# A transformer block in float32: three edits to the work of the first batch (fold constant in the prologue, xn of the next batch made and turned earlier, q scaled on GpSimd)

## The chip, the cores and the metric

The kernel runs on one core of one Trainium2 chip. A time is the device time of one execution in microseconds (us). Three runs of the kernel before gave 633.22, 635.14 and 635.72 us; the median, 635.14, is the time before. Another execution was taken with the profiler, and all rows shown here come from it.

## The reference

For x of shape 8 x 1024 x 256 (batches, tokens, channels), with 16 heads of 16 channels and a hidden layer of 1024:

```python
x  = L0_attn_x
xn = (x - mean(x)) / sqrt(var(x) + 1e-5)                    # over the 256 channels
# linear attention, no softmax
q, k, v = split(xn @ qkv_w + qkv_b)                         # 16 heads of 16
q, k = q / |q|, k / |k|                                     # per token and head
kv   = einsum('bhnd,bhne->bhde', k, v)
attn = einsum('bhnd,bhde->bhne', q, kv) @ proj_w + proj_b
# feed forward
ffn  = relu(xn @ W1 + b1) @ W2 + b2
out  = x + attn + ffn
```

Everything is float32.

## The kernel before

Batches are worked through one after the other, and each is software-pipelined with the next. A batch is 1024 tokens by 256 channels, which is eight tiles of 128 tokens.

*What is made of a batch.* `norm_stats`, `norm_scale` and `norm_apply` turn x into xn with tokens on the partitions. A turned copy `xnT`, with channels on the partitions, is made in one of two ways. For batch 0, TensorE transposes (`turn_on_pe`). For later batches `turn` (L289) is used: VectorE transposes 32 x 32 blocks into a tile `turn_x`, and DMA transfers then put the blocks where they belong. One call of `turn_x` (L304) does one of four such pieces: one VectorE transpose of 128 x 512 and four transfers of 64 KB. `project` makes q and k (products `pq`, L328, with the bias added on VectorE, L332). `norms` takes the inverse lengths and scales k on GpSimd (L464, called from `scale`); `scale_q` scales q by the same line.

*Attention without v.* v is never formed. `mix_g` (L497) multiplies the xn of a batch with its scaled k into `gp` (16 products, L502), and ScalarE copies it to `gT` (L507). `mix_kv` multiplies the v columns of `qkv_w` with `gT` (`kvp`, L516) and VectorE keeps the blocks on the diagonal (`kvm`, L522). `mix_m` multiplies with `proj_w` (`mp`, L533) into a 256 x 256 matrix M, which the second layer applies to the turned q, beside W2. The bias of v comes in by two small steps, done once. `shift` (L492) adds 1 to the first 128 channels of xn on ScalarE, and `fold_bias_of_v` (L479) changes the v columns of `qkv_w`: a product of a constant matrix `mean` (all 1/128) with these columns (`of_rows`, L485), a row `a` from it and from the bias (L487), and a sum of `a` into the columns (L490). The constant is filled by a VectorE memset (L483) in that function.

*The hidden layer.* The products of both layers use Strassen's scheme on 2 x 2 blocks, seven products for eight. In `hidden` (L543) each of four slices i has three steps: `first(i)` with the products a, c, d, `fifth(i)` with e, and `last(i)`, which adds a second product into a, d and e. Their names in the profile are `pha`, `phc`, `phd` and `phe` (L555). VectorE adds the intermediate sums u1, u2, u3 (L567) and ScalarE takes the relu (L562). GpSimd forms the sums of blocks that the second layer needs (`sums_of_h`, L188 to L192). A float32 product of 128 x 512 is two passes in the profile, hence two matmul records.

*What sets the order.* The kernel is written under a manual schedule: each engine executes its instructions in the order in which the Python code calls them, and waits by semaphore for the inputs, or for a buffer to come free. In `hidden` the twelve steps stand in a list: first(0), fifth(0), first(1), last(0), fifth(1), first(2), last(1), fifth(2), first(3), last(2), fifth(3), last(3), numbered 0 to 11. After step n come the sums of h that are due, and then the small work that a table names for n: `first_steps` (L635) for batch 0, `later_steps` for the others. So the table decides where the small products, the normalisation of the next batch and its turns stand in each engine's queue. In batch 0, the turns of batch 1 stand at steps 7, 8, 8 and 9. After `hidden(0)` come the transposes of q of batch 0 on TensorE (`tpq`, L283), GpSimd's sums of W2 (L184) and of q, `project(1)`, and then the second layer of batch 0, `second` (L684, products L679).

*Buffers that matter here.* The pool `one` has one buffer per tag. The tiles xn of all batches share the tag `xn`, so the next batch's xn may be written only when all readers of the last one, gp among them, are done. `mean`, `kvm` and `Mt` share the tag `Mt`. The PSUM tiles of the products share seven banks, taken in turn; a product that takes a bank waits until its last reader is done.

*Queues of transfers.* Nearly all transfers are issued by SyncE (SP), in order. The exception is the turns of batch 1: of the four transfers of each piece, the last is issued by ScalarE (`last`, L289 and L308).

Of the kernel before, what the change touches and what calls it, by code (L numbers as in the profile page):

```python
# [9 lines left out]
F32 = mybir.dt.float32  # L10
# [6 lines left out]
def kernel(  # L17
# [34 lines left out]
    nc = tc.nc  # L52
    P = 128
# [11 lines left out]
    R = P // S  # L65
# [7 lines left out]
    one = ctx.enter_context(tc.tile_pool(name="one", bufs=1))  # L73
# [16 lines left out]
    def bank(shape, name):  # L90

        return psum.tile(shape, F32, tag="bank", name=name)

    xs, xqs, xns, xnTs, xSs, hTs, qks, qTs, mixes, Ms, hSs = ({} for _ in range(11))
# [13 lines left out]
    def load_squares(b, halves=(0, 1)):  # L108
        xqs[b] = one.tile([P, 2, R, HT, CJ], F32, tag="xq", name=f"xq_{b}")
        for n in halves:  # L110
            for j in range(R):
                nc.sync.dma_start(out=xqs[b][ts(j, S), n], in_=squares_v(x, b, n, j))
# [51 lines left out]
    nc.vector.memset(eps_sb, LN_EPS)  # L164
    ones = const.tile([P, 1], F32, tag="ones", name="ones")
    nc.vector.memset(ones, 1.0)

    blk = const.tile([P, G], F32, tag="blk", name="blk")
    nc.vector.tensor_reduce(blk, ident.rearrange("p (g d) -> p g d", d=D), AX.X, ALU.add)
# [69 lines left out]
    def norm_stats(b, tiles):  # L239

        xt, n = xs[b], len(tiles)
        st = work.tile([P, NT, 6], F32, tag="st", name=f"st_{b}_{tiles[0]}")[:, :n, :]
        mv = small.tile([P, NT, 2], F32, tag="mv", name=f"mv_{b}_{tiles[0]}")[:, :n, :]
        for i, t in enumerate(tiles):
            nc.vector.bn_stats(st[:, i, :], xt[:, t, :])
        for i in range(n):
            nc.vector.bn_aggr(mv[:, i, :], st[:, i, :])
        rstd = small.tile([P, NT], F32, tag="rstd", name=f"rstd_{b}_{tiles[0]}")[:, :n]
        nc.scalar.activation(rstd, mv[:, :, 1], AF.Sqrt, bias=eps_sb)
        for i, t in enumerate(tiles):  # L250
            stats[b, t] = i, mv, rstd

    def norm_scale(b, tiles, on_act):
        i, mv, rstd = stats[b, tiles[0]]
        nc.vector.reciprocal(rstd, rstd)
        if on_act:
            nmr = small.tile([P, NT], F32, tag="nmr", name=f"nmr_{b}_{i}")[:, : len(tiles)]
            nc.vector.scalar_tensor_tensor(nmr, mv[:, :, 0], -1.0, rstd, ALU.mult, ALU.mult)
            for t in tiles:
                stats[b, t] += (nmr,)  # L260

    def norm_apply(b, tiles):
        if b not in xns:
            xns[b] = one.tile([P, NT, C], F32, tag="xn", name=f"xn_{b}")
        for t in tiles:
            xt, xn = xs[b][:, t, :], xns[b][:, t, :]
            i, mv, rstd, *nmr = stats.pop((b, t))
            if nmr:
                nc.scalar.activation(  # L269
                    xn, xt, AF.Identity, bias=nmr[0][:, i : i + 1], scale=rstd[:, i : i + 1]  # L270
                )
            else:
                nc.vector.tensor_scalar(
                    xn, xt, mv[:, i, 0:1], rstd[:, i : i + 1], ALU.subtract, ALU.mult
                )
# [10 lines left out]
                    tp.rearrange("p (u w) m -> p u w m", w=2),  # L286
                )

    def turn(dst, src, name, last=nc.sync):  # L289


        sq = one.tile([P, R, KC, NP, S, 2], F32, tag="turn", name=f"turn_{name}")
        src = src[:, :, 0:C].rearrange("p (u w) (k j s) -> p j k u w s", w=2, k=KC, s=S)
        for j in range(R):
            nc.vector.transpose(sq[:, j, :, :, :, :].rearrange("p k u s w -> p k u w s"), src[:, j])  # L295
            for r in range(R):
                (last if r == R - 1 else nc.sync).dma_start(
                    out=dst[ts(j, S), :, :, ts(r, S), :], in_=sq[ts(r, S), j, :, :, :, :]
                )
            yield  # L300

    turns = {}

    def turn_x(b):  # L304

        if b not in xnTs:
            xnTs[b] = big.tile([P, KC, NP, P, 2], F32, tag="xnT", name=f"xnT_{b}")
            turns["x", b] = turn(xnTs[b], xns[b], f"x_{b}", nc.scalar if b == 1 else nc.sync)  # L308
        next(turns["x", b])

    def project(b, between={}, with_norms=True):
# [42 lines left out]
    def norms(b, h, ss):  # L354
        invert(ss)
        scale(nc.gpsimd, b, h, 1)
# [104 lines left out]
    def scale(eng, b, h, s):  # L461

        part = qks[b][:, ts(h, HT), ts(s, C)].rearrange("p t (g d) -> p t g d", d=D)
        eng.tensor_tensor(  # L464
            part, part,
            norms_of[b, h, s].unsqueeze(3).to_broadcast([P, HT, H, D]), ALU.mult,
        )

    def scale_q(b, h):
        scale(nc.vector, b, h, 0)  # L470

    def turn_q(b):

# [5 lines left out]
    def fold_bias_of_v():  # L479

        wv = wqkv_sb[:, :, of_v]
        mean = one.tile([P, P], F32, tag="Mt", name="mean")
        nc.vector.memset(mean, 1.0 / P)  # L483
        of_rows = bank([P, C], "of_rows")
        nc.tensor.matmul(of_rows, mean, wv[:, 0, :], start=True, stop=True)  # L485
        a = one.tile([P, C], F32, tag="ksum", name="a")
        nc.vector.scalar_tensor_tensor(  # L487
            a, qkvb_sb[:, of_v], 1.0 / P, of_rows, ALU.mult, ALU.subtract
        )
        nc.vector.tensor_tensor(wv, wv, a.unsqueeze(1).to_broadcast([P, KC, C]), ALU.add)  # L490

    def shift(b):  # L492

        part = xns[b][:, :, 0:P]
        nc.scalar.activation(part, part, AF.Identity, bias=ones)

    def mix_g(b):  # L497
        qk, xn = qks[b], xns[b]
        gp = ps_mix.tile([P, KC, C], F32, tag="mix", name=f"gp_{b}")
        for f in range(KC):  # L500
            for t in range(NT):
                nc.tensor.matmul(  # L502
                    gp[:, f, :], xn[:, t, ts(f, P)], qk[:, t, C : 2 * C],
                    start=(t == 0), stop=(t == NT - 1),
                )
        gT = one.tile([P, KC, C], F32, tag="gT", name=f"gT_{b}")
        nc.scalar.copy(gT, gp)  # L507
        mixes[b] = gT

    def mix_kv(b):  # L510
        gT = mixes.pop(b)
        kvp = ps_mix.tile([P, KC, P], F32, tag="mix", name=f"kvp_{b}")
        for c in range(KC):
            cols = slice(2 * C + c * P, 2 * C + (c + 1) * P)
            for f in range(KC):
                nc.tensor.matmul(  # L516
                    kvp[:, c, :], wqkv_sb[:, f, cols], gT[:, f, ts(c, P)],
                    start=(f == 0), stop=(f == KC - 1),
                )
        kvm = one.tile([P, KC, P], F32, tag="Mt", name=f"kvm_{b}")  # L520
        for c in range(KC):
            nc.vector.tensor_tensor(  # L522
                kvm[:, c, :].rearrange("p (g d) -> p g d", d=D),
                kvp[:, c, :].rearrange("p (g d) -> p g d", d=D),
                blk.unsqueeze(2).to_broadcast([P, G, D]), ALU.mult,
            )
        mixes[b] = kvm

    def mix_m(b):
        kvm = mixes.pop(b)  # L530
        mp = ps_mix.tile([P, KC, C], F32, tag="mix", name=f"mp_{b}")
        for c in range(KC):
            nc.tensor.matmul(mp[:, c, :], kvm[:, c, :], projw_sb[:, c, :], start=True, stop=True)  # L533
        M = one.tile([P, KC, C], F32, tag="M", name=f"M_{b}")
        Mt = one.tile([P, 3, HC], F32, tag="Mt", name=f"Mt_{b}")
        Ms[b] = M, Mt
        nc.vector.tensor_copy(M, mp)
        sums_of_b(
            nc.gpsimd, [M[:, k, ts(m, HC)] for k in range(2) for m in range(2)],
            [Mt[:, i, :] for i in range(3)],  # L540
        )
# [93 lines left out]
    def first_steps(b):  # L635

        lo, hi = range(HT), range(HT, NT)
        return {
            0: [lambda: load_squares(b)] + [lambda h=h: norms(b, h, all_ss[b, h]) for h in range(2)],
            1: [lambda: norm_stats(b + 1, lo)],  # L640
            2: [lambda: shift(b), lambda: norm_stats(b + 1, hi), lambda: norm_scale(b + 1, lo, True)],
            3: [lambda: fold_bias_of_v()],
            4: [
                lambda: mix_g(b), lambda: norm_scale(b + 1, hi, False),
                lambda: norm_apply(b + 1, lo), lambda: scale_q(b, 0), lambda: scale_q(b, 1),
            ],
            5: [lambda: norm_apply(b + 1, hi)],
            6: [lambda: mix_kv(b)],
            7: [lambda: turn_x(b + 1)],
            8: [lambda: turn_x(b + 1), lambda: turn_x(b + 1)],  # L650
            9: [lambda: turn_x(b + 1)],
            10: [lambda: mix_m(b)],
            11: [lambda: load(b + 2)],
        }
# [236 lines left out]
```

## Time and profile before

| what | value |
|---|---|
| median of three runs | 635.14 us (633.22 to 635.72) |
| the profiled execution: its time | 633.63 us |
| the profiled execution: its span, first to last instruction | 631.8 us |
| mean granted clock of TensorE | 0.994 |
| TensorE busy | 616.4 us, 98% of the span |
| VectorE / ScalarE / GpSimd busy | 400.4 / 208.8 / 349.0 us |
| TensorE's share of the chain that ended last | 94% |

In the profile PE is TensorE, PEld its weight loads, DVE VectorE, ACT ScalarE, POOL GpSimd and SP SyncE. A row of the timeline has the start in us from the span's start, the length in us, the engine, the line of the kernel, the operation, out<-in by the program's names, the shapes, and how many instructions were merged. Brackets hold the idle time of the engine before the row, and what ended it. Lengths of merged matmuls include the tail of the last one, so the next matmul starts before a row's end. The chain of waits, the waits of an engine and the windows (busy time of each engine in a stretch, with the clock that TensorE was granted, 1.00 being full) are other views of the same execution.

### The profile page before, as it was taken

To read this page: it belongs to the slowest core of one execution; us is meant where nothing else is said; L and a number is where in the kernel's file an instruction comes from. 1 tells how busy PE (TensorE), PEld (TensorE's weight loads), DVE (VectorE), ACT (ScalarE), POOL (GpSimd) and SP (SyncE) were. 2 spreads that over 40 slices of the span, in tenths; PEclk is the share of its full clock that TensorE was granted. 3 is DMA by queue.
4 is the path that set the end of the run, shared out by engine and by line. 5 is a ranking of instruction groups with operands and counts; after the bars stand their busy time and mean duration, and the time that the engine had idled before them with its cause. 6 is when DMAs were issued, how large, how long until landed. Compare 5 with 4: busy or idle time off the path is not lost.

```text
span 631.8 us, 6102 instructions
## 1 busy us (share of the span) xinstructions
PE 616.4 (98%) x1843; PEld 346.4 (55%) x1843; DVE 400.4 (63%) x700; ACT 208.8 (33%) x348; POOL 349.0 (55%) x288
## 2 busy tenths in 40 slices
PE   8969899999999999999999999999999999999996
PEld 5445446448464475545664475644846547554454
DVE  6775553687466784577665875668746778417823
ACT  4324622343232521435214442325324252103500
POOL 3543875379702995239932599027970299513801
PEclk9979999999999999999999999999999999999999
DMA  7721300384005810158002750039200560004202
GB/s 243 141 41 22 112 1 0 78 184 73 0 7 127 168 33 1 31 125 164 14 1 58 149 126 0 2 94 192 49 0 12 122 124 11 0 0 101 66 0 66
DMA packets 139503, 43.26 MB, mean 68 GB/s; under 512 B 135880, under 2 KB 136272, under 8 KB 139472
## 3 DMA queue, kind: packets, MB, share of 16 engines
q1 hardware_dynamic: 138384, 42.63, 30.5%
q10 hardware_dynamic: 1088, 0.26, 0.2%
q8 instruction: 14, 0.23, 0.1%
q14 instruction: 17, 0.14, 0.1%
HBM read 19.80 MB, written 8.39 MB: 45 GB/s over the span
## 4 chain that ended last, share of the span: by engine, by line
PE 94%; DVE 3%; DMA 1%; ACT 0%; issue 0%; SPq 0%; DVEq 0%; ACTq 0%
PE poe L679 11%; PE poa L679 11%; PE pod L679 10%; PE gp L502 9%; PE phe L555 8%; PE phd L555 8%; PE pha L555 8%; PE poc L679 5%; PE pq L328 4%; PE phc L555 4%; PE pqd L396 3%; PE pqe L396 3%; PE pqa L396 3%; PE pqc L396 2%; PE kvp L516 1%; PE mp L533 1%
## 5 line engine op out<-in xcount | busy, mean ns | idle before, releaser
L716 POOL TENSOR_TENSOR xq<-xq,yt_o 128x512 f32<-128x512 f32 x30 | 37.9, 1264 | 180.9 <-DVE yt_o L711 180.9
L562 ACT ACTIVATE hT<-hT,b_sb 128x512 f32<-128x512 f32 x96 | 68.7, 721 | 63.4 <-DVE hT L567 59.1
L188 POOL TENSOR_TENSOR hS<-hT 128x512 f32<-128x512 f32 x31 | 46.1, 1489 | 68.6 <-issue 41.5
L555 PE MATMUL pha<-xnT,w_sb 128*128 128x512 f32 x128 | 65.4, 592 | 0.0
L374 ACT ACTIVATE sq<-qk 128x512 f32<-128x512 f32 x48 | 29.0, 629 | 109.1 <-DVE qk L402 59.1
L502 PE MATMUL gp<-qk,xn 128*128 128x256 f32 x256 | 58.0, 386 | 0.0
L679 PE MATMUL poa<-hT,w_sb 128*128 128x512 f32 x128 | 57.5, 592 | 0.0
L502 PEld LDWEIGHTS gp<-qk,xn 128*128 128x128 f32 x256 | 49.8, 195 | 11.0 <-issue 3.9
L567 DVE TENSOR_TENSOR hT<-phe,u 128x512 f32<-128x512 f32 x64 | 43.7, 683 | 6.2 <-PE phe L555 4.4
L711 DVE STREAM_TRANSPOSE yt_o<-y_o 128x512 f32<-128x512 f32 x30 | 33.0, 1099 | 16.2 <-ACT y_o L766 13.9
L190 POOL TENSOR_TENSOR hS<-hT,hS 128x512 f32<-128x512 f32 x31 | 39.9, 1286 | 2.4
L192 POOL TENSOR_TENSOR hT<-hT 128x512 f32<-128x512 f32 x31 | 40.9, 1321 | 0.0
L189 POOL TENSOR_TENSOR hS<-hS,hT 128x512 f32<-128x512 f32 x31 | 39.5, 1274 | 2.4
L567 DVE TENSOR_TENSOR u<-phc,u 128x512 f32<-128x512 f32 x32 | 21.8, 681 | 27.2 <-ACT u L581 18.1
L679 PEld LDWEIGHTS poa<-hT,w_sb 128*128 128x128 f32 x128 | 24.3, 190 | 25.0 <-issue 24.4
L295 DVE STREAM_TRANSPOSE turn_x<-xn 128x512 f32<-128x512 f32 x28 | 17.7, 685 | 31.3 <-ACT xn L269 31.3
L555 PEld LDWEIGHTS pha<-xnT,w_sb 128*128 128x128 f32 x128 | 23.8, 190 | 23.4 <-issue 21.0
L562 ACT ACTIVATE hT<-pha,b_sb 128x512 f32<-128x512 f32 x32 | 21.8, 682 | 36.8 <-PE pha L555 32.7
L555 PE MATMUL phe<-xS,w1t 128*128 128x512 f32 x64 | 33.6, 607 | 0.0
L581 ACT COPY u<-pha 128x512 f32<-128x512 f32 x32 | 18.4, 575 | 44.6 <-PE pha L555 43.9
L555 PE MATMUL phe<-xS,w_sb 128*128 128x512 f32 x64 | 32.7, 592 | 0.0
L555 PE MATMUL phd<-xnT,w_sb 128*128 128x512 f32 x64 | 32.7, 592 | 0.0
(165 smaller groups left out, 1189.9 us busy)
## 6 DMA issues: line engine op xcount, KB each, us to landing
xq<-in_L_attn_x_dram SPq DMA_DIRECT2D x60, 128.0 KB, 3.7
out_dram<-xq SPq DMA_DIRECT2D x60, 128.0 KB, 2.8
x<-in_L_attn_x_dram SPq DMA_DIRECT2D x14, 512.0 KB, 5.1
qT<-turn_q SPq DMA_DIRECT2D x112, 64.0 KB, 2.3
xnT<-turn_x SPq DMA_DIRECT2D x108, 64.0 KB, 2.1
x<-in_L_attn_x_dram SPq DMA_DIRECT2D x4, 256.0 KB, 4.5
w_sb<-in_L_ffn_W_dram SPq DMA_DIRECT2D x2, 512.0 KB, 7.4
w_sb<-in_L_ffn_W_dram SPq DMA_DIRECT2D x8, 128.0 KB, 3.1
```

The costliest lines, as they stand in the source:

```text
L188: eng.tensor_tensor(s1, a21, a22, ALU.add)
L189: eng.tensor_tensor(s2, s1, a11, ALU.subtract)
L190: eng.tensor_tensor(s4, a12, s2, ALU.subtract)
L192: eng.tensor_tensor(a21, a11, a21, ALU.subtract)
L396: nc.tensor.matmul(dst[:, w, :], a[:, g, :, w], rhs, start=start and w == 0, stop=stop, skip_group_check=True,)
L502: nc.tensor.matmul(gp[:, f, :], xn[:, t, ts(f, P)], qk[:, t, C : 2 * C], start=(t == 0), stop=(t == NT - 1),)
L555: nc.tensor.matmul(dst, lhsT, rhs, start=start, stop=stop, skip_group_check=True)
L562: nc.scalar.activation(block(i, n, m), src, AF.Relu, bias=b1_sb[:, fc : fc + 1])
L567: nc.vector.tensor_tensor(dst, p, q, ALU.add)
L679: nc.tensor.matmul(dst, l, r, start=start and n == 0, stop=stop and n == len(lhs) - 1, skip_group_check=True,)
L711: nc.vector.transpose(yt.rearrange("p u w r c -> p u r w c"), y.rearrange("p u (s r) w -> p u r w s", r=R),)
L716: nc.gpsimd.tensor_tensor(xh, xh, yt.rearrange("p u w r c -> p (u w) r c"), ALU.add)
```

## The change

The constant `mean` is filled in the prologue. In the table of batch 0, q is scaled at step 1 and on GpSimd (before: step 4, on VectorE); `fold_bias_of_v` moves from step 3 to step 4, behind fifth(1); at step 4 both halves of xn of batch 1 are written before `fold_bias_of_v` and `mix_g` are called (before: `mix_g` first, then the first half of xn, and the second half at step 5). The turns move from steps 7, 8, 8, 9 to 5, 5, 6, 7. All transfers of the turns are issued by SP.

```diff
@@ prologue
     nc.vector.memset(ones, 1.0)
+    mean = one.tile([P, P], F32, tag="Mt", name="mean")
+    nc.vector.memset(mean, 1.0 / P)
@@ turn
-    def turn(dst, src, name, last=nc.sync):
+    def turn(dst, src, name):
...
-                (last if r == R - 1 else nc.sync).dma_start(
+                nc.sync.dma_start(
@@ turn_x
-            turns["x", b] = turn(xnTs[b], xns[b], f"x_{b}", nc.scalar if b == 1 else nc.sync)
+            turns["x", b] = turn(xnTs[b], xns[b], f"x_{b}")
@@ scale_q
-        scale(nc.vector, b, h, 0)
+        scale(nc.gpsimd if b == 0 else nc.vector, b, h, 0)
@@ fold_bias_of_v
-        mean = one.tile([P, P], F32, tag="Mt", name="mean")
-        nc.vector.memset(mean, 1.0 / P)
@@ first_steps
-            1: [lambda: norm_stats(b + 1, lo)],
+            1: [
+                lambda: norm_stats(b + 1, lo), lambda: scale_q(b, 0), lambda: scale_q(b, 1),
+            ],
             2: [lambda: shift(b), lambda: norm_stats(b + 1, hi), lambda: norm_scale(b + 1, lo, True)],
-            3: [lambda: fold_bias_of_v()],
             4: [
-                lambda: mix_g(b), lambda: norm_scale(b + 1, hi, False),
-                lambda: norm_apply(b + 1, lo), lambda: scale_q(b, 0), lambda: scale_q(b, 1),
+                lambda: norm_scale(b + 1, hi, False), lambda: norm_apply(b + 1, lo),
+                lambda: norm_apply(b + 1, hi), fold_bias_of_v, lambda: mix_g(b),
             ],
-            5: [lambda: norm_apply(b + 1, hi)],
-            6: [lambda: mix_kv(b)],
+            5: [lambda: turn_x(b + 1), lambda: turn_x(b + 1)],
+            6: [lambda: mix_kv(b), lambda: turn_x(b + 1)],
             7: [lambda: turn_x(b + 1)],
-            8: [lambda: turn_x(b + 1), lambda: turn_x(b + 1)],
-            9: [lambda: turn_x(b + 1)],
             10: [lambda: mix_m(b)],
             11: [lambda: load(b + 2)],
```

## The prediction

> **What bounds the kernel now.** I read the page first, then the waits of the TensorE queue, then the timeline of each engine over the first batch, then the granted clock by microsecond. The page puts TensorE at 98% busy and 94% of the chain that ended last, so only a pause of TensorE, or slow running of it, can be won back. The waits of TensorE have two entries above 1.5 us, and both are in the first batch:
>
> ```profile
> PE of_rows L485 <- DVE mean L483: 5.5, 1, 5.5
> PE pq L328 <- DMA xnT<-turn_x: 1.9, 1, 1.9
> ```
>
> (engine, line, what it waited for: total us, times, longest.) The first is the small product of `fold_bias_of_v` (L485), held by the memset of its constant. The second is the first projection of batch 1, held by the transfers that turn its xn. Where they lie, from the timelines (start us, us, ...):
>
> ```profile
> 31.31 1.02 PE L555 MATMUL phe<-xS,w_sb 128*128 128x512 f32 x2
> 37.88 1.22 PE L485 MATMUL of_rows<-wqkv_sb,mean 128*128 128x256 f32 x2 [5.55 <-DVE mean L483]
> 40.60 8.50 PE L502 MATMUL gp<-qk,xn 128*128 128x256 f32 x32
> 48.94 1.02 PE L555 MATMUL pha<-xnT,w_sb 128*128 128x512 f32 x2
> ...
> 65.30 1.91 PE L283 MATMUL tpq<-ident,qk 128*128 128x128 f32 x16
> 69.12 3.25 PE L328 MATMUL pq<-wqkv_sb,xnT 128*128 128x512 f32 x7 [1.91 <-DMA xnT<-turn_x]
> ```
>
> ```profile
> 33.15 0.69 DVE L567 TENSOR_TENSOR u<-phc,u 128x512 f32<-128x512 f32 x1 [0.84 <-ACT u L581]
> ...
> 37.66 0.17 DVE L483 MEMSET mean<- 128x128 f32 x1
> ```
>
> The memset takes 0.17 us; it is late because VectorE works in order and it is behind the statistics of batch 1. The pause costs more than its length, as the granted clock shows (window, its length, busy us of PE, PEld, DVE, ACT, POOL with counts, then the clock):
>
> ```profile
> 36.00:37.00 1.00, 0.00 (x0) 0.00 (x0) 0.97 (x7) 0.74 (x2) 0.00 (x0) 0.83 0.00 0
> 37.00:38.00 1.00, 0.12 (x1) 0.12 (x1) 0.82 (x3) 1.00 (x3) 0.08 (x1) 0.50 0.00 0
> ...
> 43.00:44.00 1.00, 1.00 (x5) 0.82 (x5) 1.00 (x2) 0.00 (x0) 1.00 (x1) 0.76 0.00 0
> 44.00:45.00 1.00, 1.00 (x6) 0.90 (x5) 1.00 (x1) 0.00 (x0) 0.41 (x1) 1.00 0.00 0
> ...
> 69.00:70.00 1.00, 0.88 (x2) 0.51 (x3) 0.00 (x0) 1.00 (x3) 1.00 (x2) 1.00 0.94 373
> ```
>
> The clock falls to a half at about 36.7 us (0.83 in that window), and is whole again at about 43.75 (0.76). TensorE works from 37.88 on, so 5.88 us of its work run at half speed: 2.94 us lost. After the second pause of 1.91 us the clock is 1.00.
>
> **The change, step by step.**
>
> *The constant.* Its memset joins VectorE's prologue, where VectorE idles 1.82 us for x: 0.17 us at no cost. If that cover were gone it would cost 0.17.
>
> *TensorE up to the end of gp.* `fifth(1)` now comes ahead of the small product and waits for nothing: its two passes start at 31.31 + 0.86 = 32.17 and end their turn at 33.03 (0.43 a pass). The small product still needs a free PSUM bank. In the changed program that wait is for VectorE's u of `first(1)`: 33.15 + 0.69 = 33.84. So it starts at 33.88, and the pause is 33.88 - 33.03 = 0.85 us where it was 5.55. It took 1.01 (37.88 to the next pass at 38.89) at half clock; I take 0.55. gp would start at 34.43. Its other inputs are there: the keys scaled by GpSimd (28.85 + 3.82 = 32.67) and xn shifted by ScalarE (33.02 + 1.15 = 34.17). gp's 32 passes took 8.34 (40.60 to 48.94), partly at half clock; the same product of batch 1, at full clock, took 6.90 (100.11 to 107.01). So gp ends at 41.33, and `first(2)` starts there, not at 48.94: 7.6 us. The parts agree: 5.55 - 0.85 = 4.7 of pause and 2.94 of clock, 7.64.
>
> Here a rule is weighed. The Trainium skill, "TensorE: Matmul & The Clock Gate" (Part 1), says that the gate closes after an idle window of about 3.4 us and opens after about 3.4 us of steady work. By the rule the slow stretch costs 3.4 / 2 = 1.7 us and the step gives 6.4. By the row it is 5.88 us of slow work and 2.94 lost; I take the row. That 0.85 us of pause leaves the clock alone is read from the 1.91 us that did.
>
> *xn of batch 1 ahead of gT.* The tile xn has one buffer, so every write of batch 1's xn waits for the last pass of gp(0), wherever it stands in the list. ScalarE then does four xn, gT and u1 of `first(2)`; before, it was gT, four xn, u1:
>
> ```profile
> 49.14 0.59 ACT L507 COPY gT<-gp 128x512 f32<-128x512 f32 x1 [6.70 <-PE gp L502]
> 49.62 2.07 ACT L269 ACTIVATE xn<-x,nmr,rstd 128x256 f32<-128x256 f32 x4
> 51.60 0.56 ACT L581 COPY u<-pha 128x512 f32<-128x512 f32 x1
> ```
>
> The same sum, 3.02 us from 49.14, in another order: u1 ends at 41.53 + 3.02 = 44.55. gT ends 2.0 us later than it would (44.1), and kvp needs it at 41.33 + 6 x 0.86 = 46.5: covered by 2.4 us of products; without them each us would be TensorE's. On VectorE the other four xn (1.37, formerly after u3) and the fold of the weights (0.42, and 1.48 when it shared SBUF with GpSimd or 0.69 as the like sum of two SBUF tiles takes alone) end between 43.9 and 44.8; kvp has 1.7 us over. Of u2 of `first(2)` I so take 44.6, of u3 45.4 to 46.05, of the first turn 46.05 to 46.75. Should the xn stall on the sums of GpSimd that run until 43.1, at most 0.9 us is added (POOL's end at 43.1, four xn at 0.33, 0.4 and 0.7 against 44.6).
>
> *The turns.* Two turns go ahead of the sums of `last(1)` on VectorE and delay them by 1.3 us. The relu behind them that matters is fed by a sum ending at 50.3, and TensorE wants its bank at 52.5: covered. All 16 transfers are now SP's (four were ScalarE's, and took 2.8 us of its queue, in which no product waited). What precedes them in SP's queue had ended by 36. How SP issues:
>
> ```profile
> 57.80 9.55 SPq L297 DMA_DIRECT2D xnT<-turn_x  x12
> 112.63 11.35 SPq L297 DMA_DIRECT2D xnT<-turn_x  x16
> ```
>
> Without its waits for turns the first run has 0.66 us from issue to issue, the second (batch 2, all on SP, turns ready) 10.74 / 15 = 0.716, with two steps of 1.05. From 46.8 the last is issued at 56.7 to 57.5. The last one before was issued at 66.74 and landed at 68.88, and TensorE moved 0.24 later. So xnT is there at 59.1 to 59.9. TensorE comes to it at 41.33 + 16.36 (48.94 to 65.30) + 1.74 (sixteen transposes) = 59.43. I take 59.6: pause about 0.2 where it was 1.9. The first projection moves from 69.12 to 59.6: **9.5 us**. The two ends are 59.4 (no pause) and 60.8 (slower pitch and the 0.9 together): 9.7 and 8.3.
>
> *q on GpSimd.* VectorE loses 3.8 us of L464; GpSimd gains two of these, and has the room:
>
> ```profile
> 28.85 3.82 POOL L464 TENSOR_TENSOR qk<-qk,ss 128x1024 f32<-128x1024 f32 x2 [4.61 <-DVE ss L350]
> 37.92 1.27 POOL L188 TENSOR_TENSOR hS<-hT 128x512 f32<-128x512 f32 x1 [5.25 <-ACT hT L562]
> ```
>
> Key scaling took 3.82, so q runs from 32.67 to 36.5, inside the 5.25 idle before the sums of h. It is wanted at 57.7, by the transposes. A rule speaks against it: the Trainium skill, "SBUF — State Buffer" (SBUF: two separate sides), says that VectorE and GpSimd share a port pair that one locks for a whole instruction, so that a VectorE instruction with two SBUF inputs stands still behind GpSimd's. By the rule, a u of `first(1)` caught behind q would be up to 1.9 us late and the small product with it: gain 7.6. By the rows: that u reads PSUM and one SBUF tile, and L567 takes 0.69 beside a busy GpSimd as it does beside an idle one; bn_stats (four in 1.39 beside the key scaling, 1.40 alone) is not held either. I take nothing.
>
> *What comes after.* From 69.12 to the end TensorE's waits are below 0.5 us each, so the rest moves as it is, if GpSimd's sums keep up. From the sums of `last(2)` (64.64) to the last w2t (81.89) it needs 17.25 us. These sums began 3.5 us after the products; that gives 57.0 + 17.25 = 74.2, and TensorE wants them at 59.6 + 18.1 = 77.7 (69.12 to 87.23 before). No cost, 3.5 us over.
>
> Sum against the profiled execution: 633.63 (span 631.8, 1.8 around it) - 9.5 = 624.1. The median shown, 635.14, is 1.5 above that execution: 635.14 - 9.5 = **625.6**.
>
> **The rivals.**
>
> *The transfers stay late.* SP with 16 issues has no margin: for it are the two steps of 1.05 and the tie at 59.4 against 59.1 to 59.9; against it that turns begin 10 us earlier. If up to the whole 1.9 stays, the gain is 7.6: 627.5.
>
> *The clock falls anyway, or the lock bites.* With the pause of 0.85 stretched to 2.8 by the lock the gain is 7.6; if the clock also falls there, 2.9 less, 4.7: 630.4. Against: the rows above.
>
> *It does not do what it says.* gp waits for another input and the pause only changes its name: under 3 us are won, 632.5 or so. The inputs' ends (32.67, 34.17) speak against it.
>
> *Slower.* One mechanism: SP's queue. Were the pitch 1.35 us, the last transfer would land at 46.8 + 20.3 + 2.4 = 69.4, TensorE would stand for 10 us, the clock would fall and cost another 2.9: 3.2 later than now, 638.3. It decides from a pitch of 1.13 on (break-even: 66.2 + 2.9 = 69.1). Single steps of 1.05 are seen, a mean of 0.72.
>
> **How the numbers follow.** Forecast 76%, late transfers 12%, clock or lock 6%, no effect 3%, slower 3%. Faster by over 0.5% (3.2 us, about what a measurement of this kernel can tell from no change): the first three, 0.94; within: 0.03; slower: 0.03. The range: 633.22, the fastest run, less 9.7 is 623.5 at the low end; the late-transfer case at 627.5 with 1.2 us of the runs' spread is 628.7 at the high end. That leaves out the smaller part of the second rival and the last two.
>
> **What would show it.** The small product with under 1.2 us of idle before it; granted clock 1.00 from 33 to 48; gp some 6.9 long, `first(2)` at 41 to 42; xn of batch 1 waiting for gp on both engines; GpSimd's q scaling between 32 and 37; the first pq of batch 1 at 59 to 61, with under 1 us of idle. Wrong it would be by a new entry in TensorE's waits above 2 us: kvp for the weights' fold or gT, pq for turn_x, or a clock of 0.5 in that stretch.

## The result: 623.88 us, and the profile after

The changed kernel takes 623.88 us (median of four runs, 623.79 to 624.22). Four runs of the kernel before, beside it, gave a median of 635.03. The ratio is 0.983 with an interval of 0.9809 to 0.9851: 11.1 us less. The forecast was 625.6, in a range of 623.5 to 628.7. The profiled execution took 624.22 (span 622.1), against 633.63 (span 631.8): 9.4 to 9.7 us less, where the steps gave 9.5. The profile thus moved by what was worked out, and the median by 1.6 more. The experiments below show where most of that can come from.

TensorE's longest waits, in the view of waits of the changed kernel (engine, what, for what: total us, times, longest):

```profile
PE warm L794 <- POOL ident masks.py:199: 1.4, 1, 1.4
PE tpx L285 <- DVE xn L275: 1.2, 2, 1.0
PE of_rows L485 <- DVE u L567: 0.7, 1, 0.7
```

The entries of 5.5 us (`of_rows` for the constant) and 1.9 us (`pq` for the turned xn) are gone. The first two here are of the start of the program, ahead of the stretch that was changed. The timeline of TensorE in the first batch:

```profile
32.16 1.02 PE L555 MATMUL phe<-xS,w1t 128*128 128x512 f32 x2
33.89 0.70 PE L485 MATMUL of_rows<-wqkv_sb,mean 128*128 128x256 f32 x2 [0.71 <-DVE u L567]
34.43 7.07 PE L502 MATMUL gp<-qk,xn 128*128 128x256 f32 x32
41.33 1.02 PE L555 MATMUL pha<-xnT,w_sb 128*128 128x512 f32 x2
...
46.48 1.05 PE L516 MATMUL kvp<-gT,wqkv_sb 128*128 128x128 f32 x8
...
57.68 1.91 PE L285 MATMUL tpq<-ident,qk 128*128 128x128 f32 x16
59.43 2.75 PE L330 MATMUL pq<-wqkv_sb,xnT 128*128 128x512 f32 x6
```

`of_rows` waits 0.71 us for VectorE's u, as forecast, in place of 5.55 for the constant. `gp` runs from 34.43 to the start of `pha` at 41.33, 6.90 us, so at full clock. The first `pq` of batch 1 starts at 59.43 with no wait. From there to the end of the span it is 622.1 - 59.43 = 562.7 us, and before it was 631.8 - 69.12 = 562.7: all of the gain in the profile lies ahead of this product. The granted clock (last column but two) stays whole where it was a half before:

```profile
33.00:34.00 1.00, 0.29 (x2) 0.11 (x2) 0.75 (x2) 1.00 (x2) 1.00 (x1) 1.00 1.01 180
...
37.00:38.00 1.00, 1.00 (x6) 0.88 (x5) 1.00 (x3) 1.00 (x3) 0.08 (x1) 1.00 0.00 0
```

VectorE, ScalarE, GpSimd and SP's issues behind `gp`:

```profile
41.53 2.43 DVE L275 TENSOR_SCALAR xn<-x,mv,rstd 128x256 f32<-128x256 f32 x4 [3.17 <-PE gp L502]
43.88 0.41 DVE L487 SCALAR_TENSOR_TENSOR a<-qkvb_sb,of_rows 128x256 f32<-128x256 f32 x1
44.33 0.69 DVE L490 TENSOR_TENSOR wqkv_sb<-wqkv_sb,a 128x512 f32<-128x512 f32 x1
...
46.33 1.30 DVE L297 STREAM_TRANSPOSE turn_x<-xn 128x512 f32<-128x512 f32 x2
```

```profile
41.58 2.07 ACT L271 ACTIVATE xn<-x,nmr,rstd 128x256 f32<-128x256 f32 x4 [2.51 <-issue]
43.56 0.56 ACT L507 COPY gT<-gp 128x512 f32<-128x512 f32 x1
44.03 0.58 ACT L581 COPY u<-pha 128x512 f32<-128x512 f32 x1
```

```profile
28.84 7.61 POOL L466 TENSOR_TENSOR qk<-qk,ss 128x1024 f32<-128x1024 f32 x4 [4.61 <-DVE ss L352]
...
41.84 1.32 POOL L194 TENSOR_TENSOR hT<-hT 128x512 f32<-128x512 f32 x1
```

```profile
47.06 10.52 SPq L299 DMA_DIRECT2D xnT<-turn_x  x16
```

VectorE's four xn took 2.43 us, 1.06 more than before. GpSimd's four scalings, two of them of q, ended at 36.45. SP's first issue came at 47.06 and its last at 56.98, and by the trace that transfer landed at 59.11. Where TensorE waits for these transfers it starts 0.24 us after the landing (68.88 and 69.12 in the kernel before). That gives 59.35 here, and TensorE came to the product at 59.43: there was 0.08 us to spare.

### The profile page after: what moved, and what is told of

It reads as the page before. It is cut to its first block, busy times and chain, and to the rows that moved or that the text cites. A ratio compares the mean times of both kernels' runs of the same rounds, so it can differ in the third digit from the quotient of the medians.

```text
span 622.1 us, 6098 instructions
## 1 busy us (share of the span) xinstructions
PE 612.8 (98%) x1843; PEld 344.2 (55%) x1843; DVE 398.8 (64%) x698; ACT 209.0 (34%) x348; POOL 351.1 (56%) x290
## 4 chain that ended last, share of the span: by engine, by line
PE 96%; DVE 2%; DMA 1%; ACT 0%; issue 0%; SPq 0%; DVEq 0%; ACTq 0%
PE poe L678 11%; PE poa L678 11%; PE pod L678 10%; PE gp L502 9%; PE pha L555 8%; PE phe L555 8%; PE phd L555 8%; PE poc L678 6%; PE pq L330 5%; PE phc L555 4%; PE pqe L398 3%; PE pqa L398 3%; PE pqd L398 3%; PE pqc L398 2%; PE kvp L516 1%; PE mp L533 1%
## 5 line engine op out<-in xcount | busy, mean ns | idle before, releaser
L678 PE MATMUL poa<-hT,w_sb 128*128 128x512 f32 x128 | 57.5, 592 | 0.0
L502 PE MATMUL gp<-qk,xn 128*128 128x256 f32 x256 | 56.6, 379 | 0.0
L555 PE MATMUL phc<-xS,w1t 128*128 128x512 f32 x64 | 32.7, 592 | 0.0
```

Source lines behind the costliest of these rows:

```text
L502: nc.tensor.matmul(gp[:, f, :], xn[:, t, ts(f, P)], qk[:, t, C : 2 * C], start=(t == 0), stop=(t == NT - 1),)
L555: nc.tensor.matmul(dst, lhsT, rhs, start=start, stop=stop, skip_group_check=True)
L678: nc.tensor.matmul(dst, l, r, start=start and n == 0, stop=stop and n == len(lhs) - 1, skip_group_check=True,)
```

## The experiments

The experiments ran in three groups, each with runs of the kernel before on the same chip. The medians of before in these groups were 633.55 (12 runs), 633.84 (9) and 634.06 (9). They are lower than the 635.03 of the four runs beside the changed kernel. The changed kernel did not run in these groups, so a difference to its 623.88 is one between groups. In the second group, the kernel with the transfers as before (623.63, below) can stand in for it.

**The parts, one at a time.** The constant alone, on the kernel before:

```diff
     nc.vector.memset(ones, 1.0)
+    mean = one.tile([P, P], F32, tag="Mt", name="mean")
+    nc.vector.memset(mean, 1.0 / P)
 ...
         wv = wqkv_sb[:, :, of_v]
-        mean = one.tile([P, P], F32, tag="Mt", name="mean")
-        nc.vector.memset(mean, 1.0 / P)
```

> The kernel before with one edit: the constant is filled in the prologue, all else stays (fold at step 3, turns at 7, 8, 8, 9, four transfers on ScalarE, q on VectorE). Theory (first pause 4.7 us, its clock 2.9 us, second pause 1.9 us): the small product starts at 32.2 us, fifth(1) then waits for VectorE's u to 33.9, gp runs 34.7 to 41.6 at full clock, and the second pause of about 1.9 us stays because the turns keep their place behind gp: 7.3 us gained, 627.7. Rival 'the pause alone counts, the clock does not': 4.4 us gained, 630.6. Rival 'the gain comes from the turns': 2 us or less.

Measured: 629.43 us (629.43, 629.76, 627.33, 629.44), ratio 0.9916 (0.9894 to 0.9938), 4.1 below its before and 1.7 above the expectation. The run at 627.33 had a mean clock of 0.999, the others 0.992 to 0.996. The timeline of TensorE in the profiled one (629.43):

```profile
33.80 1.12 PE L555 MATMUL phe<-xS,w1t 128*128 128x512 f32 x2 [1.14 <-DVE u L567]
34.76 7.07 PE L502 MATMUL gp<-qk,xn 128*128 128x256 f32 x32
41.67 1.02 PE L555 MATMUL pha<-xnT,w_sb 128*128 128x512 f32 x2
...
63.18 9.24 PE L330 MATMUL pq<-wqkv_sb,xnT 128*128 128x512 f32 x17 [3.22 <-DMA xnT<-turn_x]
```

The 7.3 us up to `pha` (48.94 to 41.67) are all there. Then 1.3 go at once, because the pause for the turned xn grows from 1.91 to 3.22: the 12 issues of SP take 10.87 us here, where they took 9.55. A further part goes in the clock, by windows:

```profile
64.00:65.00 1.00, 1.00 (x3) 0.40 (x2) 0.00 (x0) 0.00 (x0) 1.00 (x2) 0.65 1.02 418
...
67.00:68.00 1.00, 1.00 (x3) 0.37 (x2) 0.00 (x0) 0.32 (x1) 0.99 (x1) 0.64 0.00 0
```

The clock is a half from about 64.3 to 67.7, so 3.4 us of work at half speed, 1.7 lost. 7.3 - 1.3 - 1.7 = 4.3, about what was measured (4.1 by the medians, 4.2 by the spans).

The rest without the constant, on the changed kernel:

```diff
-    mean = one.tile([P, P], F32, tag="Mt", name="mean")
-    nc.vector.memset(mean, 1.0 / P)
 ...
         wv = wqkv_sb[:, :, of_v]
+        mean = one.tile([P, P], F32, tag="Mt", name="mean")
+        nc.vector.memset(mean, 1.0 / P)
 ...
+            3: [fold_bias_of_v],
             4: [
 ...
-                lambda: norm_apply(b + 1, hi), fold_bias_of_v, lambda: mix_g(b),
+                lambda: norm_apply(b + 1, hi), lambda: mix_g(b),
```

> The changed kernel with the constant and the fold put back as before (memset inside the fold, fold at step 3); xn, turns, transfers and q stay changed. Theory: the first pause of 5.5 us and the clock of 0.5 behind it are back, gp ends near 48.9, and there is no pause before the projection of batch 1: 1.9 to 2.1 us gained against the kernel before, 633.0. If the parts do not add up but each needs the other: no gain, 635. If the turns carry the gain: 9 us.

Measured: 631.35 us (630.28 to 632.35, six runs), ratio 0.9957 (0.9939 to 0.9975), 2.2 less than its before. As expected, the first pause is whole and the second is gone:

```profile
37.48 1.22 PE L485 MATMUL of_rows<-wqkv_sb,mean 128*128 128x256 f32 x2 [5.55 <-DVE mean L483]
40.20 8.74 PE L502 MATMUL gp<-qk,xn 128*128 128x256 f32 x32
65.12 1.91 PE L283 MATMUL tpq<-ident,qk 128*128 128x128 f32 x16
66.87 3.61 PE L328 MATMUL pq<-wqkv_sb,xnT 128*128 128x512 f32 x8
```

The two parts alone give 4.1 and 2.2, together 6.3, and the whole gives 9.7 if its 623.88 is set against the before of the same group. Most of the 3.4 between is what the second pause costs once the first is gone: 3.2 of waiting and 1.7 of clock, 4.9, of which the turns win only 2.2 by themselves. Another 0.4 is order (`fifth(1)` ahead of `of_rows`: a wait of 0.71 instead of 1.14). So neither part is worth its full price without the other.

**What the pauses cost in clock.** First, the first pause of the kernel before filled with products that nobody reads:

```diff
         of_rows = bank([P, C], "of_rows")
+        fill = ps_mix.tile([P, KC, C], F32, tag="mix", name="fill")
+        for i in range(48):
+            nc.tensor.transpose(fill[:, i % KC, 0:P], ident, ident)
```

> The kernel before plus 48 transposes of the identity, read by nobody, in TensorE's queue ahead of the small product: they fill the first pause (48 x 0.108 = 5.2 us from 32.2 on) and move nothing else. Theory: the small product still starts near 37.9, but the clock stays at 1.00 and gp takes 6.9 us and not 8.3: 2.9 us gained with the wait as long as ever, 632.1. If the clock's fall does not come from the pause, or costs nothing: no gain, 635. If the clock is also what makes the times of the kernel before spread (633.2 to 635.7), the times of this one spread by under 0.6 us; if not, by 2 as before.

Measured: a median of 632.21 in seven runs, ratio 0.9961 (0.9946 to 0.9976). The runs fall in two heaps: 630.35, 630.52, 630.68, and 632.21 to 632.35. The profiled one is of the upper heap:

```profile
31.71 5.40 PE L487 MATMUL fill<-ident 128*128 128x128 f32 x48
37.43 0.70 PE L488 MATMUL of_rows<-wqkv_sb,mean 128*128 128x256 f32 x2 [0.31 <-DVE mean L483]
37.97 1.02 PE L558 MATMUL phe<-xS,w1t 128*128 128x512 f32 x2
38.82 7.07 PE L505 MATMUL gp<-qk,xn 128*128 128x256 f32 x32
...
66.02 9.24 PE L328 MATMUL pq<-wqkv_sb,xnT 128*128 128x512 f32 x17 [2.00 <-DMA xnT<-turn_x]
```

`gp` takes 6.9 us (38.82 to 45.73) although the small product starts hardly sooner (37.43 and 37.88), so it was the pause of TensorE that made it slow. Yet this execution is only 1.3 us faster than its before, because the clock was a half for 3.4 us (66.83 to 70.25) behind the *second* pause, of 2.0 us. The lower heap is 1.7 below. So the expected narrowing of the spread did not come, and the reading in the prediction that a pause of 1.9 us leaves the clock alone became doubtful. The second fall does not explain the whole upper heap: its runs have mean clocks of 0.994, 0.994, 0.998 and 0.997, and 3.4 us at half speed take 0.0027 off the mean, so at least the run with 0.998 (632.27) is long for another reason. That reason stays open. The kernel before, profiled once more without any change:

> The kernel before, unchanged, for one more profile. Open: the medians differ by 11.15 us, the two profiled executions by 9.4. If the slow stretch of the clock depends on where in its own period the pause falls, this profile has the same pause of 5.5 us but a slow stretch that is shorter or longer than 36.7 to 43.75, and a time that differs by half of that difference. If it is fixed, the stretch is the same within 0.2 us.

Measured: 634.27 us, mean clock 0.989. Behind the first pause the slow stretch is as long as in the first profile, 6.83 us, but it lies at 35.30 to 42.13 where it lay at 36.66 to 43.48. So 4.7 us of TensorE's work fell into it, and 5.6 in the first profile. The windows behind the second pause, which is 1.91 us as in the first profile:

```profile
69.00:70.00 1.00, 1.00 (x3) 0.36 (x2) 0.00 (x0) 0.80 (x1) 0.92 (x4) 0.72 1.04 393
70.00:71.00 1.00, 1.00 (x3) 0.48 (x2) 0.01 (x1) 0.00 (x0) 1.00 (x3) 0.50 0.69 266
```

The same program, the same pause, and this time the clock falls for 3.4 us (69.43 to 72.84). It seems to be so in a part of the executions: of the 30 runs of before in these three groups, 17 have a mean granted clock of 0.993 or 0.994 and a median of 633.46, and 13 have 0.989 to 0.991 and a median of 634.71. Against 633.46, the lower heap with the filled pause (630.35 to 630.68) is 2.9 us faster, as expected. The mean clock is a rough sign, for it also takes in the end of the program, where TensorE has no more work (in the profile of the changed kernel, a half from 618.87 to 622.1), and one run with 0.994 took 635.01. If the fall is the cause, a kernel whose second pause is filled must lose the upper heap. The kernel of the first experiment, with its 3.2 us filled:

```diff
                 pq = bank([P, 512], f"pq_{b}_{t}")
+                if b == 1 and t == 0:
+                    for z in range(24):
+                        nc.tensor.transpose(pq[:, ts(z % 4, P)], ident, ident)
```

> The kernel before with the constant in the prologue (as in e1_const_alone) and, ahead of the first projection of batch 1, 24 transposes of the identity into the bank that this projection overwrites: TensorE works (24 x 0.1125 = 2.7 us) through most of the 3.2 us that it waits there for the turned xn. The end of the pause stays where it is; only TensorE's idling changes. If the second pause costs the clock in most executions (my reading after the first two groups of runs): granted clock 1.00 from 30 to 75 us, 1.7 us less than e1_const_alone, about 627.5 beside a before of 633.7, and its runs within 0.6 us of each other. If the clock's fall in e1_const_alone has another cause (it would fall without the pause): the same as e1_const_alone, 629.2.

Measured: 627.40 us (627.13 to 627.69, five runs), ratio 0.9894 (0.9877 to 0.9911), 2.0 below the same kernel without the filling, which ran in another group (2.5 if each is set against its own before), and equal to the one run of that kernel whose clock held (627.33). The end of the wait is where it was (62.85 against 63.18, in an execution that is 0.31 us ahead already at the transposes of q):

```profile
59.49 2.78 PE L331 MATMUL pq<-ident 128*128 128x128 f32 x24
62.85 12.69 PE L333 MATMUL pq<-wqkv_sb,xnT 128*128 128x512 f32 x29 [0.58 <-DMA xnT<-turn_x]
```

and the clock behind it is whole:

```profile
65.00:66.00 1.00, 1.00 (x4) 0.45 (x3) 0.61 (x1) 0.35 (x1) 0.92 (x2) 1.00 0.56 217
```

Work that changes no result took 2 us off, by keeping TensorE busy. The loss in clock behind a short pause is shown.

The traces also show what decides whether a pause counts. In all twelve profiles, every stretch of full or half clock between two changes lasts a whole number of windows of 3.413 us: 3.41 us is one, 6.83 two, 27.31 eight, 30.72 nine, 58.03 seventeen, 587.09 a hundred and seventy-two. So the windows can be laid through a trace from any change on, and they do not begin with the program's pauses. Here is the window with the second pause of the kernel before and the one after it, first in its first profile, then in the repeat (the columns are again busy us of PE first, and the clock last but two):

```profile
67.38:70.79 3.41, 1.67 (x4) 0.90 (x5) 0.00 (x0) 3.26 (x6) 3.33 (x4) 1.00 0.79 257
70.79:74.20 3.41, 3.41 (x9) 1.57 (x8) 1.98 (x3) 1.26 (x2) 3.33 (x5) 1.00 0.24 94
```

```profile
66.02:69.43 3.41, 1.50 (x7) 0.81 (x5) 0.00 (x0) 3.41 (x7) 3.33 (x4) 1.00 0.70 214
69.43:72.84 3.41, 3.41 (x5) 1.33 (x4) 0.69 (x1) 1.00 (x2) 3.26 (x5) 0.50 0.38 150
```

In the first, the border of a window cuts 0.17 us off the pause. TensorE is idle for 1.74 us of the window (3.41 - 1.67), and the clock holds. In the second all 1.91 us lie in one window, and the next one runs at half clock. The other profiles agree: a window at full clock with at most 1.74 us of idle was always followed by full clock (1.61 and 1.4 are the next largest), and one with 1.91 or more always by half (2.00, 2.30, 2.36, 3.41). So in these traces the limit lies between 1.74 and 1.91 us of idle in one window. The way back is stricter: behind the pause of 5.55 us, windows at half clock with 0.74, 1.22 and 2.15 us of idle were followed by a second half window, and only one without idle by full clock. From this follows an estimate: if the windows lie at random to the program, a pause of 1.91 us counts in 44 to 54% of the executions (by the mean clock 13 of 30) and one of 3.22 us in 82 to 92% (three of the four runs of the first experiment).

**Where q is scaled.** On VectorE at step 4, behind the fold, on the changed kernel:

```diff
-        scale(nc.gpsimd if b == 0 else nc.vector, b, h, 0)
+        scale(nc.vector, b, h, 0)
 ...
-                lambda: norm_stats(b + 1, lo), lambda: scale_q(b, 0), lambda: scale_q(b, 1),
+                lambda: norm_stats(b + 1, lo),
 ...
                 lambda: norm_apply(b + 1, hi), fold_bias_of_v, lambda: mix_g(b),
+                lambda: scale_q(b, 0), lambda: scale_q(b, 1),
```

> The changed kernel with q of batch 0 scaled on VectorE at step 4, behind the fold, as the kernel before had it. Theory (VectorE's way from gp to the turns is the one with no margin: the last transfer lands 0.3 us before TensorE wants it): two instructions of about 1.1 us delay u2 of first(2) and the turns by 2.2 us, a pause of 2 us comes back before the projection of batch 1, perhaps 0.5 more before phd of first(3): 626.0 to 626.5. Rival 'which engine scales q does not matter': 623.9.

Measured: 625.85 us (625.70 to 626.92), ratio 0.9876 (0.9863 to 0.989), 2.0 more than the changed kernel (2.2 more than its stand-in of the same group), about as expected. VectorE and TensorE:

```profile
44.64 2.35 DVE L466 TENSOR_TENSOR qk<-qk,ss 128x1024 f32<-128x1024 f32 x2
46.91 0.68 DVE L567 TENSOR_TENSOR u<-phc,u 128x512 f32<-128x512 f32 x1
...
48.30 1.29 DVE L297 STREAM_TRANSPOSE turn_x<-xn 128x512 f32<-128x512 f32 x2
```

```profile
61.34 1.96 PE L330 MATMUL pq<-wqkv_sb,xnT 128*128 128x512 f32 x4 [1.37 <-ACT qT L286]
```

The 2.35 us of scaling push the turns from 46.33 to 48.30, and the projection with them. The profile puts the wait down to ScalarE's copies of the turned q. But SP's last transfer, issued at 58.96, landed at 61.10 by the trace, and the product starts 0.24 us later, as it does wherever it waits for the transfers. So it is the transfers. The pause of 1.37 did not bring the clock down in the profile.

On VectorE at step 1 (only the engine is changed back):

```diff
-        scale(nc.gpsimd if b == 0 else nc.vector, b, h, 0)
+        scale(nc.vector, b, h, 0)
```

> The changed kernel with q of batch 0 scaled on VectorE at step 1. Theory: it delays u of first(1) by about 1.7 us, the small product starts near 35.6, a pause of 2.5 us: 625.6 if the clock holds through it. If a pause of 2.5 us is enough for the clock to fall, up to 2.9 us more: 628.5. Rival 'no matter': 623.9.

Measured: 627.10 us (627.55, 627.14, 625.78, 627.06), ratio 0.9889 (0.9875 to 0.9903), 3.2 more than the changed kernel (3.5 more than its stand-in).

```profile
35.55 1.18 PE L485 MATMUL of_rows<-wqkv_sb,mean 128*128 128x256 f32 x2 [2.36 <-DVE u L567]
36.53 8.32 PE L502 MATMUL gp<-qk,xn 128*128 128x256 f32 x32
```

VectorE reaches its u behind the scaling, `of_rows` waits 2.36 us for it, and the clock is a half from 35.6 to 39.0. In time: 1.65 of pause and 1.7 of clock make 3.35. The one run at 625.78, with a mean clock of 0.998 against 0.995, fits a clock that held. So GpSimd's scaling is not a side matter of the change: on VectorE the same work costs 2.0 to 3.2 us in time.

**Who issues the transfers.** The last transfer of each piece on ScalarE, as before:

```diff
-    def turn(dst, src, name):
+    def turn(dst, src, name, last=nc.sync):
 ...
-                nc.sync.dma_start(
+                (last if r == R - 1 else nc.sync).dma_start(
 ...
-            turns["x", b] = turn(xnTs[b], xns[b], f"x_{b}")
+            turns["x", b] = turn(xnTs[b], xns[b], f"x_{b}", nc.scalar if b == 1 else nc.sync)
```

> The changed kernel with the last transfer of each piece of batch 1 on ScalarE, as before. Theory: the last transfer lands over 2 us earlier, TensorE had not waited for it, and ScalarE's relus behind the issues come late by 1 to 2 us, which costs 0 to 0.6: 623.9 to 624.5. Rival 'giving all transfers to SP was part of the gain': 625 or more.

Measured: 623.63 us (623.45 to 624.25), ratio 0.9839 (0.9826 to 0.9853): the same as the changed kernel. SP needs 9.88 us for 12 issues, hardly less than 10.52 for 16, since the issue that follows the first waits 2.0 us. In the instructions, SP's transfers share their completion semaphores in turn with ScalarE's: SP's second issue waits on the semaphore of the transfer that ScalarE issued at 46.66. So SP can be held by ScalarE's transfers. The last transfer lands at 58.05 where it landed at 59.11, and not the expected 2 us earlier. ScalarE's queue holds four issues again, and its relu behind the first of them starts at 48.27 where it started at 44.97, with no wait of TensorE behind it. This part of the change costs nothing and brings nothing.

**Can more be had?** The shift of xn by 1 at step 0, and the fold behind `gp`, on the changed kernel, so that `gp` follows `fifth(1)` at once:

```diff
-            0: [... norms(b, h, all_ss[b, h]) for h in range(2)],
+            0: [... norms(b, h, all_ss[b, h]) for h in range(2)] + [lambda: shift(b)],
 ...
-            2: [lambda: shift(b), lambda: norm_stats(b + 1, hi), lambda: norm_scale(b + 1, lo, True)],
+            2: [lambda: norm_stats(b + 1, hi), lambda: norm_scale(b + 1, lo, True)],
 ...
-                lambda: norm_apply(b + 1, hi), fold_bias_of_v, lambda: mix_g(b),
+                lambda: norm_apply(b + 1, hi), lambda: mix_g(b), fold_bias_of_v,
```

> The changed kernel with the shift of xn of batch 0 moved from step 2 to step 0, and the fold called behind gp. Theory: gp then starts right behind fifth(1), at 33.1 and not at 34.43, and the small product runs behind it in 0.43 us with no wait: first(2) comes 0.95 us earlier. The transfers follow gp by less[...]: they come 0.6 us earlier, and 0.3 us of pause before the projection remain. 0.65 us gained over the changed kernel, 623.2. Rival 'a chain other than TensorE's sets the end here': no gain.

Measured: 623.66 us (623.41 to 625.01, five runs), ratio 0.9843 (0.9829 to 0.9857). That can't be told from the changed kernel.

```profile
39.93 3.50 DVE L275 TENSOR_SCALAR xn<-x,mv,rstd 128x256 f32<-128x256 f32 x4 [1.77 <-PE gp L502]
```

```profile
56.51 1.91 PE L285 MATMUL tpq<-ident,qk 128*128 128x128 f32 x16
58.82 4.54 PE L330 MATMUL pq<-wqkv_sb,xnT 128*128 128x512 f32 x10 [0.41 <-ACT qT L286]
```

TensorE's transposes of q come 1.17 us sooner, but the turns only 0.53: `turn_x` starts at 45.80 (46.33), SP at 46.53 (47.06), for the four xn take 3.50 us and hold up the fold and u2 behind them. 0.41 is given back at the projection. It is put down to ScalarE's copies again, but the last transfer landed at 58.58, 0.24 us before the product. The projection so starts 0.61 us sooner than in the changed kernel (0.65 were expected), and of this the medians, 0.2 apart, show nothing clear. The changed kernel is at the point where the transfers set the pace.

Why are the xn slow? They take 1.37 us in the kernel before, where GpSimd is idle, 2.43 after and 3.50 here, and in the last two they end 0.8 and 0.5 us after GpSimd's sums of h (43.16 and 42.96). The first group of these sums on VectorE instead, on the changed kernel:

```diff
-                nc.vector if b == B - 1 and i == FH - 1 else nc.gpsimd,
+                nc.vector if (b == B - 1 and i == FH - 1) or (b == 0 and i == 0) else nc.gpsimd,
```

> The changed kernel with the first group of sums of h (four, batch 0, group 0) on VectorE in place of GpSimd, so that GpSimd is idle while VectorE makes its four xn of batch 1. If GpSimd's sums hold these xn (2.43 us where they took 1.37): they take 1.4 us again, end at 42.9 in place of 43.9, and the fold by 44.1. If the xn are slow for another reason (ScalarE writing the same tile beside them, or TensorE reading): 2.4 us stays. In time little follows either way, since u2 of first(2) waits for ScalarE's u1 until 44.6: turns 0.3 us sooner, 0 to 0.4 us less than the changed kernel; 623.3 to 623.9.

Measured: 624.61 us (623.86, 625.88, 623.74, 625.37), ratio 0.9851 (0.983 to 0.9872), and on VectorE:

```profile
39.56 0.68 DVE L194 TENSOR_TENSOR hT<-hT 128x512 f32<-128x512 f32 x1
...
41.10 1.38 DVE L275 TENSOR_SCALAR xn<-x,mv,rstd 128x256 f32<-128x256 f32 x4 [0.17 <-PE gp L502]
```

With GpSimd idle the xn take 1.38 us, though ScalarE writes the same tile beside them as before. So it is GpSimd's sums that hold them. VectorE gains 1.05 us there and then waits 1.01 for u1, as expected, so nothing follows in time in the profiled run (623.86). Two of the four runs are 1.5 and 2.0 us longer than it, at a mean clock no lower than its own (0.999 and 0.998 against 0.997), and put the median above the expected 623.3 to 623.9. What was late in them was not seen, and stays open.

## Why the prediction was right, and where a reading in it was not

*The first pause.* The small product was to start at 33.88, and started at 33.89. The wait is the named one, for VectorE's u. The step took 5.55 - 0.85 = 4.7 us, but these two are not counted alike: 0.85 is from the next product's turn, 5.55 from the end of the tail of the last one. Counted alike it is 5.55 to 0.71 us, 4.84.

*The clock around `gp`.* `first(2)` was to start at 41.33, and started at 41.33; `gp` took 6.90 as the product of batch 1 does. Filling the pause alone gave the same 6.9. The clock's term was off the other way. The prediction ends the slow stretch at 43.75, where the row's 0.76 means 0.48 us at half clock, so 43.48. That makes 5.60 us of slow work and 2.80 lost, not 5.88 and 2.94. The two slips cancel: 4.84 + 2.80 is 7.64, as 4.7 + 2.94 was, and 7.61 was measured (48.94 - 41.33).

Rule and row: the slow stretch behind the 5.55 us pause was 6.83 us long in all three profiles that have this pause, and 5.6, 4.7 and 6.1 us of work fell into it. So the lost time is 2.3 to 3.0 us, and the row was nearer than one window of the rule (1.7). The rule of "TensorE: Matmul & The Clock Gate" (Part 1) has the right unit, though: behind the shorter pauses of 2.0, 1.91, 3.22 and 2.36 us the slow stretch was 3.41 us each time it came, and 6.83 is two of these. That the rule's window runs freely, whatever the program does, agrees with the whole multiples of 3.413 us in these traces. That it asks for an idle window of about 3.4 us does not agree with them: 1.91 us of idle within one window were enough.

*xn ahead of `gT`.* No cost was the step. `gT` ended at 44.1, `kvp` started at 46.48 with no wait, and the fold of the weights was done at 45.0. Right, with 1.5 us over.

*The four xn of VectorE.* At most 0.9 us were allowed for GpSimd's sums, and none taken. They cost 1.06. Since u2 was due behind ScalarE's u1 (ended 44.61) in any case, it reached the turns as 0.3 only: 46.33 in place of 46.05. The prediction weighed the lock for too few instructions. The u and the statistics beside GpSimd's scaling were indeed not held. But the section that was cited ("SBUF — State Buffer", SBUF: two separate sides) names, beside instructions with two SBUF inputs, those in a mode that uses two ports for one input, and xn, a tensor_scalar from SBUF to SBUF, can be one of these. The runs agree: 1.38 us without GpSimd's sums beside it, 2.43 and 3.50 with them. That GpSimd's sums are the cause is shown; which mode xn ran in, and so that it is this lock, no trace shows.

*SP.* From 46.8 the last issue was to come at 56.7 to 57.5; it came at 56.98, from a start at 47.06 and with 0.66 us from issue to issue. The pause of 0.2 us became none. With 0.08 us to spare, the rival of late transfers was near.

*q on GpSimd.* To end at 36.5, ended at 36.45. No cost, as the step said; that it saves 2.0 to 3.2 us against the same scaling on VectorE in the new order was not worked out there.

*GpSimd's later sums.* 74.2 was reckoned for the last sum of W2, against a need at 77.7; it ended at 71.8.

*The sum.* 9.5 us by the steps; 9.7 by the spans, 9.6 between 623.88 and the 633.46 of those executions of before whose clock fell once. Part of the executions of before contain a second fall of the clock, worth 1.7, behind the second pause. The median of 635.03 fits such executions (634.71 among the 30 others), but the clocks of its four runs are not on record. The sentence that the pause of 1.91 us leaves the clock alone was read from one execution, and the next profile of the same kernel contradicts it. This is the term that the sum lacked: between 0 and 1.7 us, 1.25 between the medians of the two kinds of execution. The measured 623.88 lies 0.4 us above the low end of the range, and that end was set by the spread of the runs of before, not by this term: here the prediction had luck. For the pause of 0.85 the conclusion held all the same, since after 0.71 the clock was whole in the profile, and the runs of the changed kernel lie within 0.4 us of each other where those of before spread over 2.5.

## What to carry to other kernels

Price a pause of TensorE as its length plus the slow work behind it, and take the slow part from more than one execution: a pause of some 2 us cost 1.7 us in some executions and nothing in others, by where a window of 3.41 us cut it. Pauses of up to 1.37 us left the clock alone in every profile here. A wide spread of the runs can be a sign of a pause near 2 us, though some of the spread here has another cause that was not found. Where two pauses stand in a row on one engine, a shorter first one lengthens the second unless the work that feeds the second moves too: the parts gave 4.1 and 2.2 us alone, and 9.7 together. Before moving work to VectorE, look at what is queued behind it there; the same two scalings (2.35 and 2.66 us) cost 2.0 or 3.2 us on VectorE by their place, and nothing on GpSimd.

## What the runs showed of the hardware that was not expected

- Behind the pauses in mid-program, slow stretches of TensorE's clock came in two lengths only: 3.41 us (behind pauses of 1.91, 2.0, 2.36 and 3.22 us) and 6.83 us (behind 5.55 us). Behind 1.91 us it came in one of two profiles of the same kernel, and behind 0.71, 1.14 and 1.37 us in none.
- From one change of the clock to the next it was always a whole number of windows of 3.413 us. The clock fell behind every window with 1.91 us of idle or more, and behind none with 1.74 or less.
- VectorE's four normalisations of 128x256 took 1.37 us alone, 2.43 and 3.50 us beside GpSimd's sums of two SBUF tiles, and 1.38 again when these sums were taken away.
- Two scalings of 128x1024 took VectorE 2.35 us with GpSimd idle, and 3.81 (first experiment) beside GpSimd's sums, which in turn grew from 1.27 to as much as 2.24 us each. On GpSimd, ahead of these sums, a scaling took 1.9 us.
